# Spreading small vectors over the partitions of a four-layer graph network: through DRAM in place of transposes of repeated columns

## The chip, the cores and the metric

The kernel runs on one core of a Trainium2 chip. The metric is the device time of one execution in microseconds (us). Before the change it is 2883.72 us, the median of three runs (2882.16 to 2886.92).

A core has five engines with queues of their own: TensorE (PE in the profile; PEld is its weight load), VectorE (DVE), ScalarE (ACT), GpSimd (POOL) and SyncE (SP). Transfers between DRAM and the on-chip memory are issued on the queues of SP, ACT and POOL and carried out by 16 DMA engines.

## The reference

Four layers over 2708 nodes with 512 features each, all with the same adjacency `adj` (2708 x 2708, mostly zeros), in float32. Each layer adds its result to x and normalises the rows. What the change touches belongs to the first two:

```python
# layer 0: incidence = adj
mask = adj > 0
head = mask / maximum(sqrt(sum(mask * mask, axis=-1)), EPS)   # 1/sqrt(count of the row)
inc = adj + head
x = layernorm(x + (inc @ x) / sum(inc, axis=-1))
# layer 1
h = x @ W_sa
s_left, s_right = h @ a_sa[0, :512], h @ a_sa[0, 512:]        # = x @ (W_sa @ a)
attn_a = sigmoid(concat([adj @ x, x]) @ Wa.T + ba)            # attn_b alike, with Wb
e = where(adj != 0, exp(-leaky_relu(s_left[:, None] + s_right[None, :])), 0)
x = layernorm(x + sigmoid(attn_a * ((e / sum(e)) @ h) + attn_b * (adj @ (x @ W_gcnb) + b_gcnb)))
```

So layer 0 needs for each node the inverse root of its count of neighbours, and adds it to each entry of its row that is not zero. Layer 1 needs four scalar products of every node's x with fixed vectors: two score vectors (W_sa times the halves of a_sa) and the second halves of Wa and Wb.

## The kernel before

The adjacency is held transposed (`adjT`), so that a node's row is a column on the chip: 128 source nodes on the partitions, a range of target nodes along the free axis. Each product adj @ x is one level of a seven-product scheme on halves of 1354 nodes. A **sweep** goes over ranges of target nodes; for layer 0 these are (768,256), (0,384), (384,384) and (1024,330) (start within a half, length), numbered 0 to 3 here. For each range the four blocks 11, 21, 22 and 12 of `adjT` are loaded as tiles of 128 x n (SP queue, L394), combined by DVE into sums (L403; stored for later layers by POOL, L406), and multiplied on PE (L458, with the rest of the rows at L467 to L482) by parts of x: B11, B22, B21 and the sums T1 to T4 (L224 to L232), each in groups A to D of three tiles. Results gather in PSUM banks, of which there are eight under one tag.

**Order.** Nothing is issued where it stands in the code. Every step is put down as an event, `at(position, function)`; a sweep takes 28 positions per layer (`S[1]` is where layer 1's begins), and the events run sorted by position. A scheduler then moves instructions of each engine after a start-up stretch. On one queue everything runs in its order: an issue that waits holds what stands behind it. Tiles come from rings (38 for adjacency tiles, 17 called tmp, 6 masks), and a tile is overwritten when its last reader is done.

**Counts and inverse roots (layer 0).** For the next range, `count_load` (L691) loads 22 tiles per half again, on SP for range 1 and on POOL for ranges 2 and 3, ACT (L712, L713) or DVE (L710) makes masks of them, and PE multiplies each mask by a column of ones (`count_tile`, L723), so that the counts gather with the target nodes on the partitions, one column for each 128. `count_row` (L728) makes the inverse root y of them on DVE and ACT (L735 to L743, tile "r"). The entries are needed along the free axis, the same on all partitions, because DVE adds them to tiles that have the target nodes there. So `spread_row` (L746) takes each column of y, repeated 128 times along the free axis, as a matrix and transposes it on PE (L751, tile "pr"), and ACT copies the result to the tile "row" (L754). `prep0` uses it (L769, L770). Each range has two halves, h = 0 and 1, each with a spreading of its own: three transposes, or two for range 0.

**Score vectors (layer 1).** `start0` loads W_sa and the halves of a_sa, and DVE multiplies and adds them up (L842) into `vmat`, [128, 4 chunks, 4 vectors]; L845 adds the columns of Wa and Wb. Just after layer 1's sweep begins (position S[1] + 0.85), `spread_v` (L891) makes each of the 16 columns, repeated, into a 128 x 128 matrix, transposes it on PE (L897, tile "pv", four PSUM banks), and ACT copies the banks into eight 128 x 256 tiles (L900) that lie in parts of the x groups B and D that no product needs any more: B11B, B22B, T1B, T2B, T3B, B21B, B11D, B22D. `score` (L904) multiplies each tile of the new x with them on DVE (L909).

`to_rows` (L920) is an existing helper of layer 1: it transposes a few columns on PE (L923, tile "ps_r"), copies the rows on ACT (L925, tile "rows") and stores them to DRAM on POOL's queue (L926). The rows s_left so stored are read back for all partitions by SP (L1075). At the start of layer 1's sweep, the last tiles of layer 0's result are still being finished: PE transposes them back (L589, tile "ps_n"), DVE adds them to x (L824) and normalises (L553 to L567), which writes the parts of B11 that layer 1's first products read.

Of the kernel before, what the change touches and what calls it, by code (L numbers as in the profile page):

```python
# [21 lines left out]
F32 = mybir.dt.float32  # L22
# [3 lines left out]
P = 128  # L26
# [4 lines left out]
RANGES0 = [(768, 256), (0, 384), (384, 384), (1024, 330)]  # L31
# [27 lines left out]
def wt(k):  # L59
    return min(P, NH - k * P) if k < KT else P  # L60
# [8 lines left out]
def gnn_kernel(ctx: ExitStack, tc: tile.TileContext, x, adjT, w_sa, a_sa, w_gcn, b_gcn, wab, bab, w_hop, w_out,  # L69
               b_out, out):  # L70
    nc = tc.nc
    N, D = x.shape
    NT = 2 * KT
    DC = D // P
    HD = D // 2
    assert N == 2 * NH and D == 512

    const = ctx.enter_context(tc.tile_pool(name="const", bufs=1))
    feat = ctx.enter_context(tc.tile_pool(name="feat", bufs=1))
    pool = ctx.enter_context(tc.tile_pool(name="pool", bufs=1))  # L80
    small = ctx.enter_context(tc.tile_pool(name="small", bufs=6))
    psum = ctx.enter_context(tc.tile_pool(name="psum", bufs=1, space=bass.MemoryType.PSUM))
    dram = ctx.enter_context(tc.tile_pool(name="dram", bufs=1, space=bass.MemoryType.DRAM))

    ident = const.tile([P, P], F32, name="ident")
# [23 lines left out]
    wab_sb = const.tile([P, 2 * DC, 2], F32, name="wab_sb")  # L109
# [5 lines left out]
    for c in range(1, DC):  # L115
        nc.vector.tensor_tensor(pick, pick, ident[:, 32 * c : 32 * c + 2], ALU.add)
    bab_sb = const.tile([P, 2], F32, name="bab_sb")
    vmat = const.tile([P, DC, 4], F32, name="vmat")
    sc = const.tile([P, NT, 4], F32, name="sc")
    sc2 = const.tile([P, NT, 2, 4], F32, name="sc2")  # L120
    nc.vector.memset(sc2, 0.0)
# [1 line left out]
    def feature(nm):  # L123
# [6 lines left out]

    SROW = {(R0, h): dram.tile([(w + P - 1) // P, P], F32, name=f"SR{R0}_{h}", tag=f"SR{R0}_{h}")
            for R0, w in RANGES for h in range(2)}
    DROW = [dram.tile([1, KT * P], F32, name=f"DR{h}", tag=f"DR{h}") for h in range(2)]

    X2T = {(g, h): dram.tile([D, 2 * n], F32, name=f"X2T{g}_{h}", tag=f"X2T{g}_{h}")
# [6 lines left out]
    def bcast(src, n):  # L142
        return bass.AP(tensor=src.tensor, offset=src.offset, ap=[[0, P], [1, n]])
# [12 lines left out]
    def tmp(nm):  # L156
        return pool.tile([P, 384], F32, name=nm, tag="tmp", bufs=NTMP)
# [10 lines left out]
    def bank(nm, shape=None):  # L168
        return psum.tile(shape or [P, D], F32, name=nm, tag="x", bufs=8)
# [6 lines left out]
    def at(pos, fn, hold=False):  # L176

        def go():
            n = len(nc.cur_bb.bb.instructions)
            fn()  # L180
            held.update(range(n, len(nc.cur_bb.bb.instructions)))

        events.append((pos, len(events), go if hold else fn))
# [499 lines left out]
    S = [28.0 * s for s in range(8)]  # L683


    row, run, rd = {}, {}, {}
    cnt = {}
    V = {}

    def tiles_of(R0, n):  # L690
        return list(range(R0 // P, (R0 + n + P - 1) // P))  # L691

    def count_load(R0, n, h, i):
        w = wt(i % KT)
        t = tmp("cl")
        j0 = (i // KT) * NH + (i % KT) * P

        move(nc.sync if R0 == RANGES0[1][0] else nc.gpsimd, t[:w, :n], adjT[j0 : j0 + w, h * NH + R0 : h * NH + R0 + n])
        cnt[R0, h, i] = t

    def count_rows(R0, i):

        return {KT - 1: KA, NT - 1: 32}.get(i, P) if R0 == RANGES0[0][0] else wt(i % KT)
# [22 lines left out]
    def count_row(R0, n, h):  # L726


        ts = tiles_of(R0, n)
        r = small.tile([P, 4, 4], F32, name="r", bufs=2)  # L730
        ps = cnt.pop(h)
        if wt(ts[-1]) < P:
            nc.vector.memset(r[:, 0, :], 1.0)
        for j, q in enumerate(ts):
            nc.vector.tensor_scalar(r[: wt(q), 0, j : j + 1], ps[: wt(q), j : j + 1], 1.0, None, ALU.max)  # L735
        m = len(ts)

        c, y, q, t = (r[:, i, :m] for i in range(4))
        nc.scalar.activation(q, c, AF.Sqrt)
        nc.vector.reciprocal(q, q)  # L740
        nc.vector.tensor_tensor(t, q, q, ALU.mult)
        nc.vector.scalar_tensor_tensor(t, c, -0.5, t, ALU.mult, ALU.mult)
        nc.vector.scalar_tensor_tensor(y, t, 1.5, q, ALU.add, ALU.mult)  # L743
        cnt[R0, h] = r

    def spread_row(R0, n, h):  # L746
        r = cnt.pop((R0, h))
        pr = bank("pr")
        for j, q in enumerate(tiles_of(R0, n)):
            w = wt(q)  # L750
            nc.tensor.transpose(pr[:, q * P - R0 : q * P - R0 + w], r[:w, 1, j : j + 1].to_broadcast([w, P]),  # L751
                                ident[:w, :w])
        row[R0, h] = tmp("row")
        nc.scalar.copy(row[R0, h][:, :n], pr[:, :n])  # L754
# [30 lines left out]
    def extra0(pb, r, R0, n, A):  # L785
        if r == 0:
            for h, p, d in ((0, -3.7, 0.05), (1, 1.9, 0.055)):
                for j, i in enumerate([*range(KW), *range(KT, KT + KW), KT - 1, NT - 1]):
                    key = (f"{h + 1}{i // KT + 1}", i % KT) if i % KT < KW else ("r" if i < KT else "r32", h)
                    a = lambda key=key: A[(0,) + key]  # L790
                    at(pb + p + d * (j - 2 * h), lambda h=h, i=i, a=a: count_mask(R0, n, h, i, a(), h == 0 or i % KT == KT - 1))
                    at(pb + p + d * j, lambda h=h, i=i: count_tile(R0, n, h, i))
                    at(pb + (1.7 if h == 0 else 4.8) + 0.06 * j,
                       lambda h=h, i=i, a=a: add_run(R0, h, n, count_rows(R0, i), a()))
                at(pb + p + d * 22, lambda h=h: count_row(R0, n, h))
                at(pb + p + d * 22 + 0.1 * h, lambda h=h: spread_row(R0, n, h))
        if r + 1 < len(RANGES0):
            R1, n1 = RANGES0[r + 1]
            for h, p, d in ((0, 1.0, 2.5), (1, 3.8, 2.5)) if r else ((0, 3.2, 2.2), (1, 5.4, 2.1)):
                for i in range(NT):  # L800
                    q = pb + p + d * i / NT
                    at(q - 0.7, lambda i=i, h=h: count_load(R1, n1, h, i))
                    at(q - 0.35, lambda i=i, h=h: count_mask(R1, n1, h, i))
                    at(q, lambda i=i, h=h: count_tile(R1, n1, h, i))
                at(pb + p + d, lambda h=h: count_row(R1, n1, h))
                at(pb + p + d + 0.15, lambda h=h: spread_row(R1, n1, h))

        def inverse(o, s, t, w):
            nc.vector.reciprocal(o, s)

        at(pb + (5.2 if r else 3.3), lambda: run_sums(R0, n, 0, inverse))
        at(pb + (4.7 if r else 6.4), lambda: run_sums(R0, n, 1, inverse))
# [20 lines left out]
    def start0():  # L833
        ws = load_w(w_sa)
        nc.scalar.dma_start(out=wab_sb, in_=wab)
        nc.scalar.dma_start(out=bab_sb, in_=bcast(bab, 2))
        y = nat("vy")
        for n in range(2):
            v = nat("va")
            nc.scalar.dma_start(out=v, in_=bcast(a_sa[:, n * D : (n + 1) * D], D))  # L840
            for c in range(DC):
                nc.vector.scalar_tensor_tensor(y, ws[c], 1.0, v, ALU.mult, ALU.mult,  # L842
                                               accum_out=vmat[:, c, n : n + 1])
        for c in range(DC):
            nc.vector.tensor_copy(vmat[:, c, 2:4], wab_sb[:, DC + c, :])  # L845
            nc.vector.tensor_copy(wab_pad[:, c, 0:2], wab_sb[:, c, :])

    def x0_load(k, s):
# [7 lines left out]
    for k in range(KW):  # L856
        f = k / KT
# [33 lines left out]
    def spread_v():  # L891

        homes = [spare_part(s, g) for g in "BD" for s in ("B11", "B22", "T1", "T2", "T3", "B21")][:8]
        for j in range(4):
            ps = bank("pv")
            for c in range(DC):
                nc.tensor.transpose(ps[:, c * P : (c + 1) * P], vmat[:, c, j : j + 1].to_broadcast([P, P]), ident)  # L897
            for e in range(2):
                V[j, e] = homes[2 * j + e]
                nc.scalar.copy(V[j, e], ps[:, e * HD : (e + 1) * HD])  # L900

    at(S[1] + 0.85, spread_v)

    def score(t, w, got):  # L904
        x1 = got[t]
# [6 lines left out]
    def scores_end(R0, h, ts):  # L912
# [3 lines left out]
        nc.vector.tensor_copy(s_right[:, q], sc[:, q, 1])  # L916
        for j in range(2):
            nc.vector.tensor_scalar(gate_x[:, q, j], sc[:, q, 2 + j], bab_sb[:, j : j + 1], None, ALU.add)

    def to_rows(cols, m, dst):  # L920

        ps = bank("ps_r", [P, P])
        nc.tensor.transpose(ps[:m], cols, ident)  # L923
        t = small.tile([P, P], F32, name="rows", bufs=2)
        nc.scalar.copy(t[:m], ps[:m])  # L925
        nc.gpsimd.dma_start(out=dst, in_=t[:m])  # L926

    def score_rows(R0, h, ts):
        q = slice(h * KT + ts[0], h * KT + ts[-1] + 1)
# [24 lines left out]
    def extra1(pb, r, R0, n, A):  # L954
# [32 lines left out]
        def rows(h):  # L987
            to_rows(rdeg[:, h * KT + ts[0] : h * KT + ts[-1] + 1], len(ts),
                    DROW[h][0, ts[0] * P : (ts[-1] + 1) * P].rearrange("(k i) -> k i", i=P))

# [450 lines left out]
    def finish_degrees():  # L1441
        t = small.tile([24, P], F32, name="fd", bufs=1)
        nc.vector.memset(t, 1.0)
        for g, (i0, n) in enumerate(RANGES2):
            for h in range(2):
                for s in range(2):
                    r, a = 12 * g + 6 * h + 3 * s, i0 + s * n
                    nc.gpsimd.dma_start(out=t[r : r + 2], in_=DROW[h][0, a : a + 2 * P].rearrange("(k i) -> k i", i=P))
                    nc.gpsimd.dma_start(out=t[r + 2 : r + 3, : n - 2 * P], in_=DROW[h][0:1, a + 2 * P : a + n])
        ps = bank("ps_r", [P, 24])  # L1450
# [104 lines left out]
    for n, i in enumerate(list(nc.cur_bb.bb.instructions)):  # L1555
        p = last if n < 3 * strict else done if n in held else {}
# [44 lines left out]
```

## Time and profile before

| | |
|---|---|
| median of three runs | 2883.72 us |
| profiled execution | 2883.33 us |
| its span (first to last instruction) | 2881.2 us |
| mean granted TensorE clock | 0.998 |
| PE busy | 2832.7 us, 98% |
| DVE busy | 2195.9 us, 76% |
| ACT, POOL busy | 550.1 us, 617.6 us |
| moved by DMA | 510.04 MB, mean 177 GB/s |
| transposes "pr" (L751) | 22, of 273 ns median |
| copies "row" (L754) | 8, of 449 ns median |
| transposes "pv" (L897) | 16, of 273 ns median |
| copies of "pv" (L900) | 8, of 372 to 453 ns |
| transposes "ps_r" (L923) | 16, of 272 ns median |

The profile is of one execution. The duration of a matmul includes the time until its result is out, and matmuls overlap; so the time that one takes from the next is read from their starts. A timeline's line is a run of alike instructions: start, length from the first start to the last end, engine, line, operation, output, inputs, shape and number, and in brackets how long the engine was idle before it, and for whom. Layer 0's sweep lies at about 10 to 440 us, with its ranges in order; layer 1's follows, until about 830.

### The profile page before, as it was taken

How to read it: one execution, taken by the hardware profiler on the slowest of the kernel's cores; microseconds unless marked ns; L12 is line 12 of the kernel's file. 1: busy time of each engine (PE TensorE's matmuls, PEld its weight loads, DVE VectorE, ACT ScalarE, POOL GpSimd, SP SyncE). 2: the span in 40 equal slices, each digit the busy share in tenths (PEclk: the TensorE clock that was granted, in tenths of full speed). 3: DMA queues.
4: the chain of work that ended last, by engine and by line, in shares of the span. 5: the costliest groups of instructions: out<-in, count | busy, mean ns of one | idle time of the engine just before them, and what ended most of it. 6: DMA issues, size and time to landing. Idle time of an engine off the chain costs nothing. (4 is left out here: it accounts for less than half of the span.)

```text
span 2881.2 us, 37482 instructions
## 1 busy us (share of the span) xinstructions
PE 2832.7 (98%) x10963; PEld 1870.3 (65%) x10963; DVE 2195.9 (76%) x5670; ACT 550.1 (19%) x1119; POOL 617.6 (21%) x1113
## 2 busy tenths in 40 slices
PE   7999999999999999999999999999999999999998
PEld 5655665657765656866666666666666666666665
DVE  6898798576736464654699787887878877799987
ACT  4544200111136444542100000000000100100001
POOL 0123223123320101122203123031230211501202
PEclk9999999999999999999999999999999999999999
DMA  7665466354544333565667767566675666754542
GB/s 229 193 212 179 133 204 218 124 181 143 183 140 130 117 113 98 151 198 151 195 205 236 213 192 246 166 201 208 187 250 168 181 197 182 230 174 145 175 142 92
DMA packets 368524, 510.04 MB, mean 177 GB/s; under 512 B 63424, under 2 KB 321700, under 8 KB 368320
## 3 DMA queue, kind: packets, MB, share of 16 engines
q1 hardware_dynamic: 302392, 370.56, 43.5%
q0 software_dynamic: 49344, 126.38, 13.1%
q10 hardware_dynamic: 16584, 10.71, 1.3%
q8 instruction: 87, 1.43, 0.2%
q14 instruction: 117, 0.96, 0.1%
HBM read 423.77 MB, written 83.65 MB: 176 GB/s over the span
## 5 line engine op out<-in xcount | busy, mean ns | idle before, releaser
L1212 DVE TENSOR_TENSOR z<-z 128x339 f32<-128x339 f32 (+1 forms) x966 | 454.3, 503 | 12.5 <-PE accu L1267 3.2
L1285 ACT COPY q<-accu 128x338 f32<-128x338 f32 (+1 forms) x84 | 34.6, 443 | 1003.3 <-PE accu L1267 806.0
L560 POOL TENSOR_TENSOR rstd<-rstd,neg_half 128x1 f32<-128x1 f32 (+3 forms) x91 | 59.3, 652 | 762.2 <-DVE rstd L559 516.6
L1267 PE MATMUL accc<-s,t 128*128 128x338 f32 (+1 forms) x644 | 198.1, 450 | 0.0
L1267 PE MATMUL accu<-z,t 128*128 128x338 f32 (+1 forms) x644 | 194.0, 448 | 1.5 <-DVE z L1212 1.5
L1267 PE MATMUL accd<-z,t 128*128 128x338 f32 (+1 forms) x644 | 193.9, 448 | 0.6 <-DVE q L1349 0.6
L1267 PE MATMUL accc<-z,t 128*128 128x338 f32 (+1 forms) x644 | 193.5, 448 | 0.5 <-ACT q L1285 0.5
L1400 POOL DMA_DIRECT2D Y<-y x192 | 105.1, 554 | 366.3 <-DVE y L1395 333.3
L403 DVE TENSOR_TENSOR a<-a,a 128x384 f32<-128x384 f32 (+2 forms) x330 | 162.4, 510 | 23.1 <-PE accu L458 22.4
L1267 PEld LDWEIGHTS accc<-s,t 128*128 128x128 f32 x644 | 120.9, 190 | 64.1 <-issue 7.5
L1267 PEld LDWEIGHTS accc<-z,t 128*128 128x128 f32 x644 | 122.0, 190 | 61.6 <-issue 1.0
L1267 PEld LDWEIGHTS accu<-z,t 128*128 128x128 f32 x644 | 121.7, 190 | 61.7 <-DVE z L1212 2.0
L1267 PEld LDWEIGHTS accd<-z,t 128*128 128x128 f32 x644 | 121.9, 190 | 60.5 <-DVE q L1349 1.5
L1212 DVE TENSOR_TENSOR s<-z 128x338 f32<-128x338 f32 (+1 forms) x322 | 149.7, 503 | 12.7 <-PE accc L1267 8.4
L1291 DVE TENSOR_TENSOR q<-q,accd 128x338 f32<-128x338 f32 (+1 forms) x112 | 56.0, 500 | 115.2 <-PE accd L1267 115.2
L1068 DVE SCALAR_TENSOR_TENSOR a<-a,e 128x384 f32<-128x384 f32 (+2 forms) x160 | 77.4, 507 | 49.8 <-ACT e L1067 49.5
L1066 ACT ACTIVATE e<-row,s_right 128x384 f32<-128x384 f32 (+5 forms) x176 | 96.3, 569 | 76.2 <-PE accc L458 20.4
L965 DVE SCALAR_TENSOR_TENSOR deg<-a,deg 128x384 f32<-128x384 f32 (+2 forms) x152 | 75.2, 505 | 19.0 <-DMA a<-in_adjT 17.9
L406 POOL DMA_DIRECT2D As<-a x120 | 64.9, 544 | 82.3 <-DVE a L403 80.3
L1067 ACT ACTIVATE e<-e 128x384 f32<-128x384 f32 (+5 forms) x176 | 79.3, 477 | 1.8
L606 PE MATMUL ps_d<-w,xT 128*128 128x512 f32 (+1 forms) x176 | 79.2, 593 | 0.4 <-ACT xT L597 0.4
L769 DVE SCALAR_TENSOR_TENSOR s<-a,row 128x384 f32<-128x384 f32 (+2 forms) x152 | 75.0, 505 | 6.0 <-ACT row L754 6.0
(683 smaller groups left out, 5869.0 us busy)
## 6 DMA issues: line engine op xcount, KB each, us to landing
z<-As SPq DMA_DIRECT2D x320, 169.5 KB
z<-As SPq DMA_DIRECT2D x320, 169.0 KB
a<-in_adjT SPq DMA_DIRECT2D x240, 192.0 KB
z<-in_adjT SPq DMA_DIRECT2D x240, 169.5 KB
z<-in_adjT SPq DMA_DIRECT2D x240, 169.0 KB
a<-in_adjT SPq DMA_DIRECT2D x120, 165.0 KB
a<-in_adjT SPq DMA_DIRECT2D x112, 128.0 KB
As<-a POOLq DMA_DIRECT2D x60, 192.0 KB, 4.2
```

Source lines behind the costliest of these rows:

```text
L403: nc.vector.tensor_tensor(A[r, dst, k][:, :n], A[r, a, k][:, :n], A[r, b, k][:, :n], op)
L406: nc.gpsimd.dma_start(out=SD[m][k * P : (k + 1) * P, R0 : R0 + n], in_=A[r, dst, k][:, :n])
L560: nc.gpsimd.tensor_tensor(rstd[:w, 1:2], rstd[:w, 0:1], neg_half[:w], ALU.pow)
L606: nc.tensor.matmul(o, lhs(c), r, start=c == 0 and n == 0, stop=c == DC - 1, skip_group_check=True)
L769: nc.vector.scalar_tensor_tensor(t[:w, :n], a[:w, :n], 0.0, row[R0, h][:w, :n], ALU.is_gt, ALU.mult)
L965: nc.vector.scalar_tensor_tensor(d[:w, :n], a[:w, :n], 0.0, d[:w, :n], ALU.not_equal, ALU.add)
L1066: nc.scalar.activation(e[:w, :n], row[R0, h][:w, :n], AF.Prelu, bias=s_right[:w, t : t + 1], alpha=0.01)
L1067: nc.scalar.activation(e[:w, :n], e[:w, :n], AF.Exp, scale=-1.0)
L1068: nc.vector.scalar_tensor_tensor(a[:w, :n], a[:w, :n], 0.0, e[:w, :n], ALU.not_equal, ALU.mult)
L1212: nc.vector.tensor_tensor(d[:, :n], Z[x + (k,)][:, :n], Z[y + (k,)][:, :n], op)
L1267: nc.tensor.matmul(B[home][:, :n], stat(v, k), a[:, :n], start=bool(start and k == 0), stop=k == nk - 1, skip_group_check=True)
L1400: nc.gpsimd.dma_start(out=rows[:, :, f * P : (f + 1) * P], in_=o[32 * f : 32 * (f + 1), : m * P].rearrange("p (b d) -> p b d", d=P))
```

## The change

`vmat` is laid out by vector, then chunk. `to_rows` may be given a queue and is defined earlier. Two DRAM tiles are added.

- The four vectors' 16 columns are transposed in one piece, at position 10.3, soon after `start0`, and stored as 16 rows on POOL's queue. `spread_v`, now at S[1] + 0.75, issues eight loads on SP's queue, each of which reads half a vector (256 numbers) for all 128 partitions into the tile that ACT's copy wrote before.
- For the first halves (h = 0) of ranges 1 to 3, `row_out` transposes the three columns of the inverse roots in one piece and stores three rows on ACT's queue, at the position where `spread_row` was, and `row_in`, 0.45 positions later, reads them for all partitions on SP's queue. The second halves, and both halves of range 0, stay with `spread_row`.
- `count_row` sets all of the tile "r" to 1 for a range that ends in a tile of under 128 nodes, where it set only the counts.

```diff
-    vmat = const.tile([P, DC, 4], F32, name="vmat")
+    vmat = const.tile([P, 4, DC], F32, name="vmat")
...
+    VROW = dram.tile([4 * DC, P], F32, name="VR", tag="VR")
+    CROW = {R0: dram.tile([3, P], F32, name=f"CR{R0}", tag=f"CR{R0}") for R0, _ in RANGES0[1:]}
...
-            nc.vector.memset(r[:, 0, :], 1.0)
+            nc.vector.memset(r, 1.0)
...
+    def to_rows(cols, m, dst, queue=None):
+
+        ps = bank("ps_r", [P, P])
+        nc.tensor.transpose(ps[:m], cols, ident)
+        t = small.tile([P, P], F32, name="rows", bufs=2)
+        nc.scalar.copy(t[:m], ps[:m])
+        (queue or nc.gpsimd).dma_start(out=dst, in_=t[:m])
+
+    def row_out(R0, n, h):
+        r = cnt.pop((R0, h))
+        m = len(tiles_of(R0, n))
+        to_rows(r[:, 1, :m], m, CROW[R0][:m, :], nc.scalar)
+
+    def row_in(R0, n, h):
+        src = CROW[R0][0:1, :]
+        row[R0, h] = tmp("row")
+        nc.sync.dma_start(out=row[R0, h][:, :n], in_=bcast(src, n))
...
-                at(pb + p + d + 0.15, lambda h=h: spread_row(R1, n1, h))
+                if h:
+                    at(pb + p + d + 0.15, lambda h=h: spread_row(R1, n1, h))
+                else:
+                    at(pb + p + d + 0.15, lambda h=h: row_out(R1, n1, h))
+                    at(pb + p + d + 0.6, lambda h=h: row_in(R1, n1, h))
...
-                                               accum_out=vmat[:, c, n : n + 1])
+                                               accum_out=vmat[:, n, c : c + 1])
...
-            nc.vector.tensor_copy(vmat[:, c, 2:4], wab_sb[:, DC + c, :])
+            nc.vector.tensor_copy(vmat[:, 2:4, c], wab_sb[:, DC + c, :])
...
-            ps = bank("pv")
-            for c in range(DC):
-                nc.tensor.transpose(ps[:, c * P : (c + 1) * P], vmat[:, c, j : j + 1].to_broadcast([P, P]), ident)
+            src = VROW[j * DC : (j + 1) * DC, :]
             for e in range(2):
                 V[j, e] = homes[2 * j + e]
-                nc.scalar.copy(V[j, e], ps[:, e * HD : (e + 1) * HD])
-
-    at(S[1] + 0.85, spread_v)
+                nc.sync.dma_start(out=V[j, e], in_=bass.AP(tensor=src.tensor, offset=src.offset + e * HD, ap=[[0, P], [1, HD]]))
+
+    at(10.3, lambda: to_rows(vmat.rearrange("p j c -> p (j c)"), 4 * DC, VROW))
+    at(S[1] + 0.75, spread_v)
```

More of the change, by code (lines that the diff above doesn't have):

```diff
@@ L918, in scores_end @@
             nc.vector.tensor_scalar(gate_x[:, q, j], sc[:, q, 2 + j], bab_sb[:, j : j + 1], None, ALU.add)
[L920 to L926, printed above, removed]
     def score_rows(R0, h, ts):
```

## The prediction

> **What bounds the kernel now.** I read the busy shares first, then what TensorE (PE) waited for, then PE's stretches around the touched places, and only then the queues.
>
> The page's busy part, first rows:
>
> ```profile
> span 2881.2 us, 37482 instructions
> PE 2832.7 (98%) x10963; PEld 1870.3 (65%) x10963; DVE 2195.9 (76%) x5670; ACT 550.1 (19%) x1119; POOL 617.6 (21%) x1113
> ```
>
> PE is busy 98% of the span: a microsecond taken from PE's stream is a microsecond gained, unless PE then waits longer; work on other engines and queues is free until it makes PE wait. The waits of PE (engine, line, waited for: us, times, longest) name the two places that this change touches:
>
> ```profile
> PE pr L751 <- DVE r L743: 5.8, 3, 2.7
> PE accu L458 <- DVE B11D L567: 3.1, 2, 2.1
> ```
>
> The first is the wait for an inverse root, before the transposes that spread it; the longest of the three (2.7) is range 1's first half. The second stands right behind the transposes of the score vectors, as PE's timeline shows:
>
> ```profile
> 441.68 4.03 PE L458 MATMUL accu<-a,B11C 128*128 128x384 f32 x12
> 445.55 1.91 PE L897 MATMUL pv<-ident,vmat 128*128 128x128 f32 x16
> 449.53 1.56 PE L458 MATMUL accu<-a,B11D 128*128 128x384 f32 x4 [2.06 <-DVE B11D L567]
> ```
>
> PE ends the sixteen transposes at 447.46, then idles 2.06 us until VectorE (DVE) has written B11D. Who makes B11D late is in DVE's timeline:
>
> ```profile
> 444.31 0.56 DVE L965 SCALAR_TENSOR_TENSOR deg<-a,deg 128x384 f32<-128x384 f32 x1 [6.41 <-DMA a<-in_adjT]
> ...
> 449.06 0.41 DVE L567 TENSOR_SCALAR B11D<-ld,mv,rstd 128x256 f32<-128x256 f32 x1
> ```
>
> DVE stands idle 6.41 us for one adjacency tile, and runs without a break from its landing to B11D. No transpose of the score vectors is in this chain.
>
> The third thing to see is the granted clock (start:end, us, PE, PEld, DVE, ACT and POOL busy, PEclk, DMA share, GB/s) around the 2.73 us wait at 89.42 to 92.14:
>
> ```profile
> 90.00:91.00 1.00, 0.00 (x0) 0.00 (x0) 0.96 (x5) 0.10 (x1) 0.00 (x0) 0.92 0.96 315
> 91.00:92.00 1.00, 0.00 (x0) 0.00 (x0) 0.63 (x5) 0.88 (x3) 0.00 (x0) 0.50 0.60 187
> ...
> 96.00:97.00 1.00, 1.00 (x7) 0.64 (x5) 1.00 (x4) 0.97 (x3) 0.00 (x0) 0.50 0.70 183
> 97.00:98.00 1.00, 1.00 (x5) 0.87 (x4) 1.00 (x4) 0.89 (x2) 0.00 (x0) 0.67 0.42 128
> ```
>
> The clock falls to 0.50 about 1.4 us into the idle time (0.92 in the first slice) and stays there some 6.8 us (0.16 + 6 + 0.66). PE works 5.5 of these at half rate, so it loses 2.75 us beside the wait itself. The 2.06 us wait at 447 costs no clock: the slice 445.5 to 449.5 has 1.00.
>
> **What goes.** PE loses 25 transposes. The three groups of the first halves (ranges 1, 2, 3) stand at 92.14, 178.14 and 284.25. At 178.14 three take 0.33 us until the next matmul (0.11 each); at 92.14, at half clock, 0.70. So 0.70 + 0.33 + 0.33 = 1.36 us leave PE. The sixteen at 445.55 take 16 x 0.11 = 1.76 us, but the next matmul waits for B11D, which does not depend on them: their going only lengthens the wait from 2.06 to about 3.85 us (445.68 to 449.53). I count 0. ScalarE (ACT) loses 11 copies of 0.37 to 0.48; it is at 19%, so 0.
>
> **What comes on PE.** Four transposes of 2 to 16 columns (one for each range, one for all score vectors). The nearest rows, the same helper's for degrees and scores, last 0.27 us each, drain included; the time a transpose takes from the next matmul is 0.11, as above (0.22 at half clock). 0.22 + 3 x 0.11 = 0.55, bounds 0.45 and 1.1. I take 0.55. Each still waits for the same root or vector: range 1's wait stays 2.73 us, with its slow clock; the vectors' last product ends on DVE at 173.58, and the transpose's place in the built order is about 174.27, so 0.7 us of cover; without cover, up to the row of such a wait, 2.7.
>
> **The clock behind the longer wait.** A wait of 3.85 us is longer than the 2.73 that halved the clock. Bounds: 0 (as after 2.06) and 2.75 (as after 2.73). If the clock falls 1.4 us into the wait for 6.8 us, it is low from 447.1 to 453.9. The four matmuls from 449.53 take 2.6 us instead of 1.3, until 452.1; but PE stood idle from 451.09 to 452.09 there for the next B11D, so that is hidden. From 452.1 to 453.9, 1.8 us at half rate lose 0.9. I take +0.9. [...]
>
> **What comes on the queues.** Three ACT-issued stores, one POOL-issued store, eleven loads on SP (three rows of 165 to 192 KB, eight vector halves of 128 KB): 1.6 MB of 510, on DMA engines busy 58%. Small stores of the same helper land in 1.5 / 1.8 / 5.4 us (least, median, most). What counts is that a queue is in order: an issue that waits holds everything behind it. I went through the changed kernel's instruction order place by place, with the old times:
> - Range 1's row load stands on SP ahead of eight count loads (issued 87.63 to 96.5). The root comes at 92.1, so the round trip ends about 95.5, and SP stands some 8 us. The loads then go out by about 100.6; their masks start on ACT from 104.68: 4 us of cover. The row is first used at 102.51, and lands near 99.
> - Ranges 2 and 3: SP stands 2.6 us at 179.7 and under 1 us at 286; users start 1.5 us or more later.
> - The vectors' store makes POOL stand from about 161.5 to 175.5, ahead of four count loads issued at 164 to 166 before. They land about 180 to 181; ACT needs them from 183.1. Cover 2 to 3 us.
> - Each vector half overwrites a tile that PE still reads, so SP waits for PE. The longest is the first: B11B waits from about 336.4 to 347.14, 10.7 us, with some ten issues behind it (338.6 to 349.96, to go out by 352.4); DVE uses them from 352.66 on, cover 2 to 5 us, and PE uses DVE's output later still. Others (T1B, T2B, B22B, B22D, B21B) move loads by 0.6 to 4.4 us, with users 4 us or more behind.
>
> I take 0 for all of them: PE has no wait on a DMA there, and SP waits of 20.3 us (longest of 82 on one line) are in the profile with PE at 98%. Without cover, each costs what PE's waits for DVE cost in the rows above, 1.0 to 2.7 us.
>
> **One wait moves by itself.** SP's transfers take completion counters in turn, shared with ACT's, and wait for the one before on the same counter. At 434.57 SP stood for that:
>
> ```profile
> SPq L297 <- DMA B11R<-X: 4.1, 1, 4.1
> ```
>
> The added transfers shift whose turn it is. By the new order the tile that DVE waits for at 444.31, issued at 435.25, waits for a transfer that lands about 438.5. It landed 9 us after its issue, behind a full DMA load, so 3.3 us later at issue are less at landing: between -1 (other loads are out of its way) and +3. I take +0.5, since the backlog in front of it, not its issue, set its time.
>
> **Sum**, against the profiled execution (2883.33 us, span 2881.2): 2883.33 - 1.36 + 0.55 + 0.9 + 0.5 = **2883.9**. The median shown is 2883.72, so this is no difference that can be seen: about 0.2%, 5.8 us, is what a measurement of this kernel can tell from no change.
>
> **Rivals.**
> - *Faster: the tile lands early.* If DVE's tile comes 4 us sooner, B11D is ready when PE gets there: 3.85 us of wait go, the clock stays up, and with -0.81 the time is 2883.33 - 3.85 - 0.81 = 2878.7; if range 1's slow clock is avoided as well (2.75), 2875.9. For it: the chain is set by that one landing. Against: the tile is issued later, not earlier. 0.20, of which 0.12 past 0.2%.
> - *Slower: SP's wait for PE at the vector halves.* If tiles held behind B11B, T1B, T2B, B22B and B22D land after DVE wants them, PE starves by 1.0 to 2.7 us at each (the bounds above): five times 1.8, about 9, with PE then at work where the slow clock was counted (0.9), gives 2883.9 - 0.9 + 9 = 2892. It decides from the point where a held tile takes over 2 us (the thinnest cover) from issue to landing; the small stores' most is 5.4, the tile above took 9. Against: PE has DVE's output in hand. 0.22, of which 0.18 past 0.2%.
> - *Nothing changes*: all of it is hidden, the clock too: 2883.33 - 0.81 = 2882.5. 0.08.
> - Forecast: 0.50, own range 2881 to 2888.
>
> **Numbers.** Faster 0.12; same 0.50 + 0.08 + 0.08 + 0.04 = 0.70; slower 0.18. The range runs from 2877.5 (into the faster case) to 2891 (into the slower one), leaving about 0.1 on each side.
>
> **What would show it.** Right: no pr groups at 178 and 284, accu behind 445.7 idle 3 to 4 us for B11D, a granted clock near 0.5 in 450 to 454, and no new wait of PE between 340 and 430. Wrong: PE waiting on DVE a (L403, L770) with DVE waiting on DMA there (slower rival); B11D early (faster rival); a wait at the score transpose near 174 or for a count mask near 183; clock 1.00 behind the long wait.

## The result, and the profile after

The changed kernel takes 2887.64 us (median of 20 runs, 2884.27 to 2893.5); the kernel before, timed beside it, 2883.44 us (median of 20, 2877.94 to 2886.92). The ratio is 1.0015, with a 95% interval of 1.0009 to 1.0021: 0.15% slower, 2.6 to 6.1 us. The profiled execution took 2888.78 us. All profiled spans below are single executions, and one kernel's differ by several us; so times are compared by ratios, and profiles by the waits that they show.

The page's busy part after the change:

```profile
span 2887.0 us, 37440 instructions
PE 2834.3 (98%) x10942; PEld 1869.5 (65%) x10942; DVE 2195.7 (76%) x5670; ACT 548.4 (19%) x1112; POOL 617.4 (21%) x1114
```

PE has 21 matmuls fewer, and is busy 1.6 us longer: some of its work ran at a lower clock (mean granted 0.996, for 0.998 before). Its waits (engine, line, waited for: us, times, longest):

```profile
PE ps_n L591 <- DVE P1c L521: 4.6, 1, 4.6
PE accu L460 <- DVE B11D L569: 3.5, 1, 3.5
...
PE ps_r L751 <- DVE r L745: 2.7, 1, 2.7
PE accd L460 <- DVE a L405: 2.5, 3, 1.9
```

The longest wait for a root (ps_r) is as long as the one for pr was: a row is now one small transpose, behind the same wait. The wait for B11D grew. The longest, for P1c, is one that the prediction does not mention. It was there before, at 2 us, as PE's timeline of the kernel before shows:

```profile
436.14 0.74 PE L589 MATMUL ps_n<-ident,P1c 128*128 128x128 f32 x2 [1.98 <-DVE P1c L519]
```

After the change, the same work and what follows:

```profile
439.71 0.88 PE L591 MATMUL ps_n<-ident,P1c 128*128 128x128 f32 x2 [4.58 <-DVE P1c L521]
...
454.14 5.49 PE L460 MATMUL accu<-a,B11D 128*128 128x384 f32 x8 [3.53 <-DVE B11D L569]
```

The eight matmuls behind B11D take 5.49 us, where two groups of four took 1.56 each before. The clock is the reason (start:end, us, PE, PEld, DVE, ACT, POOL busy, PEclk, DMA share, GB/s):

```profile
440.00:441.00 1.00, 1.00 (x5) 0.88 (x5) 1.00 (x4) 0.00 (x0) 0.26 (x2) 0.50 0.46 130
...
453.00:454.00 1.00, 0.00 (x0) 0.00 (x0) 0.85 (x2) 0.00 (x0) 0.56 (x1) 0.55 0.00 0
...
457.00:458.00 1.00, 1.00 (x3) 0.54 (x2) 0.87 (x3) 0.00 (x0) 0.95 (x2) 0.50 0.39 152
...
459.00:460.00 1.00, 1.00 (x2) 0.46 (x2) 0.54 (x2) 0.33 (x1) 0.53 (x1) 0.53 0.08 16
```

It is halved behind both waits: 3.4 us long behind the first (0.28 x 2 + 2 + 0.43 x 2, from the slices 439 to 443), 6.8 us behind the second.

Who makes P1c late? DVE's timeline before, and then after, at the sum that needs the third tile of B22's group C:

```profile
420.80 0.42 DVE L225 TENSOR_TENSOR T2C<-B22C,T1C 128x256 f32<-128x256 f32 x1 [0.26 <-DMA B22C<-X]
```

```profile
358.94 0.50 DVE L789 SCALAR_TENSOR_TENSOR s<-a,row 128x330 f32<-128x330 f32 x1 [1.10 <-DMA a<-in_adjT]
...
424.37 0.43 DVE L227 TENSOR_TENSOR T2C<-B22C,T1C 128x256 f32<-128x256 f32 x1 [2.86 <-DMA B22C<-X]
...
439.16 0.90 DVE L521 TENSOR_TENSOR P1c<-P1c,acca 128x330 f32<-128x330 f32 x2
...
448.92 0.56 DVE L980 SCALAR_TENSOR_TENSOR deg<-a,deg 128x384 f32<-128x384 f32 x1 [7.12 <-DMA a<-in_adjT]
```

DVE waits 1.10 us for an adjacency tile that it never waited for, and 2.6 us longer for B22C. From there on it runs into P1c with no pause but one of 0.46 us, which it had before as well. The tile B22C is loaded by POOL, whose issues come 0.96 us later (417.77 for 416.81), as everything does behind the first wait; from issue to landing (least, median, most) it took, before and after:

```profile
DMA to landing us min/median/max: 2.7/2.9/2.9
```

```profile
DMA to landing us min/median/max: 5.1/5.5/5.5
```

And SP stands where the prediction said, by its own waits after the change between 336 and 372:

```profile
SPq L922 <- PE accu L460: 10.7, 1, 10.7
SPq L922 <- PE accd L460: 6.8, 1, 6.8
```

**Where the time came from.** The start of the same matmul in both profiles, after minus before, tells where PE falls behind. It is +0.48 at 58 us (from the first loads, not the change) and -0.16 at 340: -0.19 is a shorter wait for DVE at 58, and -0.45 comes between 60 and 340, where the groups of pr went and the small transposes came. From there:

| place on PE | after - before | step |
|---|---|---|
| 340 | -0.16 | |
| T1C, behind DVE's 1.10 us wait at 358.9 | +0.97 | +1.13 |
| ps_n, wait for P1c | +3.57 | +2.60 |
| accu B11B, slow clock behind it | +4.90 | +1.33 |
| accu B11D, behind DVE's tile at +4.61 | +4.61 | -0.29 |
| accc T3B, slow clock behind it | +6.20 | +1.59 |
| ps_r of the degrees, whose wait of 0.60 goes | +5.44 | -0.76 |
| last matmul | +5.58 | +0.14 |

The steps are PE's, and not each is a cost. DVE's tile in front of B11D (the line at 448.92, 444.31 before) came 4.61 us later, and it alone sets when B11D is ready: the 1.33 us of the slow clock behind P1c only made PE's wait for it shorter.

### The profile page after: what moved, and what is told of

Same layout as the page of the kernel before. It is cut to its first block, busy times and chain, and to the rows that moved or that the text cites. A ratio compares the mean times of both kernels' runs of the same rounds, so it can differ in the third digit from the quotient of the medians.

```text
span 2887.0 us, 37440 instructions
## 1 busy us (share of the span) xinstructions
PE 2834.3 (98%) x10942; PEld 1869.5 (65%) x10942; DVE 2195.7 (76%) x5670; ACT 548.4 (19%) x1112; POOL 617.4 (21%) x1114
## 5 line engine op out<-in xcount | busy, mean ns | idle before, releaser
L1227 DVE TENSOR_TENSOR s<-z 128x338 f32<-128x338 f32 (+1 forms) x322 | 149.6, 503 | 10.7 <-PE accc L1282 8.2
```

What stands on the lines that cost most here:

```text
L1227: nc.vector.tensor_tensor(d[:, :n], Z[x + (k,)][:, :n], Z[y + (k,)][:, :n], op)
```

## The experiments

Theory: (1) the score vectors' loads among layer 0's last loads make B22C and adjacency tiles late, through SP's hold, their bytes or both; (2) the missing transposes only lengthen the wait for B11D; (3) behind a longer wait the clock is halved. Rivals: the rows' round trips are the loss; or PE's work counts and the loss is something else. Each kernel ran 8 to 11 times beside 15 to 30 runs of the kernel before on the same chip; ratios are to that.

**Only the rows** (twice). In the changed kernel:

```diff
-            src = VROW[j * DC : (j + 1) * DC, :]
+            ps = bank("pv")
+            for c in range(DC):
+                nc.tensor.transpose(ps[:, c * P : (c + 1) * P], vmat[:, j, c : c + 1].to_broadcast([P, P]), ident)
...
-                nc.sync.dma_start(out=V[j, e], ...)
+                nc.scalar.copy(V[j, e], ps[:, e * HD : (e + 1) * HD])
...
-    at(10.3, lambda: to_rows(vmat.rearrange("p j c -> p (j c)"), 4 * DC, VROW))
-    at(S[1] + 0.75, spread_v)
+    at(S[1] + 0.85, spread_v)
```

> The rows of the first halves through DRAM as in the change; the score vectors by transposes as before. My theory now (the loss lies with the score vectors' loads and with the slow clock behind longer waits; the rows are worth a little): time 0.5 us below before, ratio 0.9998; PE's waits at 436 and 449 as before (about 2.0 and 2.1), clock 1.00 behind them. Rival (the rows' round trips hold the queues and cost the time): 3 to 5 us above before, with the waits at 436 and 449 as long as after the change (4.6 and 3.5).

> The variant with only the rows through DRAM, a second time, since it came out 3.4 us faster than before (interval 0.9 to 6.1) where my terms gave 0.5. If that is so: ratio again near 0.9988. [...]

Ratios 0.9988 (0.9979 to 0.9997) and 0.9992 (0.9983 to 1.0000): faster than before, by 3.5 and 2.3 us in the middle, the second 0.0004 above what was expected. P1c's wait is 2.3 and 2.1 us. The rival is out: the rows are no loss. The gain is larger than my 0.5 us, which the second interval takes in and the first (from 0.9 us) just does not. The two profiles of this one kernel differ by 4.9 us of span, and show why a single profile cannot settle it. The clock near range 1, first profile, then second:

```profile
85.00:86.00 1.00, 1.00 (x6) 0.77 (x5) 0.97 (x4) 0.97 (x4) 0.00 (x0) 0.50 1.03 320
...
94.00:95.00 1.00, 1.00 (x9) 0.80 (x8) 0.93 (x4) 0.97 (x3) 0.00 (x0) 1.00 0.24 77
```

```profile
85.00:86.00 1.00, 1.00 (x9) 0.80 (x8) 0.97 (x4) 0.97 (x3) 0.00 (x0) 1.00 0.98 343
...
94.00:95.00 1.00, 1.00 (x4) 0.73 (x3) 0.93 (x4) 0.97 (x3) 0.00 (x0) 0.50 0.20 69
```

In one the clock fell behind the wait of 2.02 us at 81 and stayed up behind the one at 89, which was only 1.82 us long there; in the other it stayed up behind 2.02 us and fell behind 2.74 us at 88, for twice as long. In the second it also fell for 6.8 us behind the wait for B11D (2.83 us), against the expectation of 1.00 there.

**Only the score vectors.** The changed kernel with `spread_row` for all halves.

> The score vectors through DRAM as in the change; all rows by transposes as before. My theory: 4 to 5.5 us above before, ratio about 1.0017; DVE waits about 1 us for an adjacency tile near 358 and 2 to 3 us for B22C near 421, PE waits over 4 us for P1c near 436 and over 3 us for B11D, and the granted clock is 0.5 behind both. Rival (the rows are the loss): within 1 us of before, or 1 to 2 below it.

Ratio 1.0031 (1.0020 to 1.0042), 9 us: more than expected, and enough for all of the loss. The profile is of a run of 2897.0 us, above the median of 2891.71. DVE waited 3.0 us for B22C, PE 4.7 us for P1c and 4.7 for B11D, and the clock was 0.50 behind both.

**Fifteen of the sixteen transposes taken from the kernel before.**

```diff
-            ps = bank("pv")
-            for c in range(DC):
-                nc.tensor.transpose(ps[:, c * P : (c + 1) * P], vmat[:, c, j : j + 1].to_broadcast([P, P]), ident)
+        # once, ahead of the loop over j
+        ps = bank("pv")
+        nc.tensor.transpose(ps[:, :P], vmat[:, 0, 0:1].to_broadcast([P, P]), ident)
...
-                nc.scalar.copy(V[j, e], ps[:, e * HD : (e + 1) * HD])
+                nc.scalar.copy(V[j, e], ps[:, 0:1].to_broadcast([P, HD]))
```

> The kernel before, with one of the sixteen transposes of the score vectors; the eight copies spread that one result, so fifteen of the sixteen columns are left out. No transfer is added. My theory (these transposes stand in a wait that something else ends): the wait for B11D grows from 2.1 to about 3.7 us, and the time stays or grows by up to 2.7 us, by the slow clock behind the longer wait (granted clock 0.5 for some 3 to 7 us from about 449). Rival (PE is busy 98%, so its work counts): 1.65 us below before (15 x 0.11).

Ratio 0.9997 (0.9988 to 1.0006): no gain is seen, though the interval would hold one of 1.65 us (0.9994), so the time alone decides nothing. The profile shows where the work went, in PE's timeline and the clock:

```profile
445.76 0.27 PE L895 MATMUL pv<-ident,vmat 128*128 128x128 f32 x1
451.03 5.38 PE L458 MATMUL accu<-a,B11D 128*128 128x384 f32 x8 [5.00 <-DVE B11D L567]
```

```profile
452.00:453.00 1.00, 1.00 (x3) 0.51 (x2) 0.41 (x3) 0.00 (x0) 0.87 (x2) 0.50 0.84 61
```

The wait took the work's place (of its 5.00 us some 1.3 are because B11D came later in this execution), and the clock fell to 0.50 behind it, with no transfer added.

**The transposes put back into the changed kernel, unread.**

```diff
+            ps = bank("pv")
+            for c in range(DC):
+                nc.tensor.transpose(ps[:, c * P : (c + 1) * P], vmat[:, j, c : c + 1].to_broadcast([P, P]), ident)
             src = VROW[j * DC : (j + 1) * DC, :]
```

> The changed kernel, with the sixteen transposes put back at their old place for PE alone: nobody reads them, and the vectors still come from DRAM. My theory: not slower than the changed kernel though PE does 1.76 us more; the wait for B11D falls from 3.5 to about 1.8 us, the clock behind it stays 1.00, and the time falls by 1 to 2.5 us against the changed kernel (2 to 3.5 us above before). The wait for P1c near 436, over 4 us, and the late B22C stay. Rival (PE's work counts): 1.8 us above the changed kernel, 6 above before.

Ratio 1.0009 (1.0000 to 1.0017), against 1.0015 for the changed kernel. The intervals overlap, so a gain is not shown; a loss of 1.8 us (to 1.0021) is just outside. P1c's wait is still 4.6, but behind B11D the clock stays up:

```profile
455.08 1.56 PE L460 MATMUL accu<-a,B11D 128*128 128x384 f32 x4 [1.42 <-DVE B11D L569]
457.52 1.56 PE L460 MATMUL accu<-a,B11D 128*128 128x384 f32 x4 [0.89 <-DVE B11D L569]
```

**The vectors' loads kept at their place in the list**, on SP behind layer 0's last loads (the third argument keeps the scheduler from moving an event's instructions):

```diff
-    at(S[1] + 0.75, spread_v)
+    at(S[1] + 0.75, spread_v, True)
```

> The changed kernel, with the eight loads of the score vectors kept at their place in the list of events, after the last tiles of layer 0's end on SP's queue, so that SP does not wait for PE between 336 and 430 and none of these loads is under way with B22C. My theory (the loads among layer 0's last loads make B22C and the adjacency tile late): DVE's wait for B22C under 1 us, PE's wait for P1c about 2, no clock loss there; what is left is the longer wait for B11D with a slow clock behind it; 1 to 3 us above the variant that has only the rows, so -2.5 to +1 us against before. Rival (the missing transposes before the wait for B11D are the whole loss, by the clock): about as the changed kernel, +4.

Ratio 0.9996 (0.9987 to 1.0005): the loss is gone. B22C lands after 2.9 us again, DVE waits 0.3 for it, and what is left is the longer wait and a slow clock behind it:

```profile
PE accu L460 <- DVE B11D L569: 4.6, 1, 4.6
PE ps_n L591 <- DVE P1c L521: 2.0, 1, 2.0
```

```profile
450.00:451.00 1.00, 1.00 (x2) 0.42 (x2) 0.40 (x2) 0.00 (x0) 0.88 (x2) 0.50 0.74 235
```

**The same, with the transposes put back, unread** (the edit as above).

> The variant with the vectors' loads kept at their place, with the sixteen transposes put back at their old place for PE alone, unread. My theory (the clock falls behind the longer wait): PE's wait for B11D falls from 4.6 to about 2.8 us or is split in two, the clock stays 1.00 or is slow for fewer us behind it, and the time is the same or up to 1.5 us lower though PE does 1.76 us more. Rival (PE's work counts): 1.76 us higher.

Ratio 0.9998 (0.9989 to 1.0007): 1.76 us more PE work, no difference that can be seen, though the intervals would hold one of that size. The clock is 1.00 from 446 to 452, behind waits of 2.83 and 0.89 us.

**Is it the one place in DRAM, the queue, or the bytes?** Three kernels. The vectors' rows stored sixteen times, and read from sixteen places:

```diff
-    VROW = dram.tile([4 * DC, P], F32, name="VR", tag="VR")
+    VROW = dram.tile([16, 4 * DC, P], F32, name="VR", tag="VR")
...
-                nc.sync.dma_start(out=V[j, e], in_=bass.AP(..., ap=[[0, P], [1, HD]]))
+                nc.sync.dma_start(out=V[j, e], in_=bass.AP(..., ap=[[4 * D, 16], [0, 8], [1, HD]]))
...
+        nc.gpsimd.dma_start(out=VROW.rearrange("r q i -> q r i"), in_=t[: 4 * DC].unsqueeze(1).to_broadcast([4 * DC, 16, P]))
```

> The changed kernel, with the vectors' rows stored sixteen times in DRAM, so that a load of one half reads sixteen different places and not one for all 128 partitions. If reading one place 128 times is what holds up B22C: DVE's wait for it falls from 2.9 to under 1 us, PE's wait for P1c from 4.6 to about 2, and the time falls by 2 to 4 us against the changed kernel (0 to 2 above before). If it is only that these and the held loads come just then: as the changed kernel, 4 to 5 us above before, with waits of 2.9 and 4.6.

Ratio 1.0024 (1.0014 to 1.0035), B22C after 5.3 us, DVE's wait 2.7, P1c's 4.4, as in the changed kernel: not the one place.

The loads on ACT's queue:

```diff
-                nc.sync.dma_start(out=V[j, e], ...)
+                nc.scalar.dma_start(out=V[j, e], ...)
```

> The changed kernel, with the eight loads of the score vectors on ACT's queue instead of SP's, at about the same times (ACT then waits for PE, and its own later work waits behind). If it is SP's hold that hurts (the loads behind it come late and close together): DVE's wait for B22C falls under 1 us, its waits for adjacency tiles near 358 go, PE's wait for P1c is about 2, and the time is near that of the variant with loads kept at their place (ratio about 0.9996 to 1.0005). If it is the vectors' transfers themselves, under way with B22C: that wait stays 2 to 3 us, P1c's over 4, and the time stays 3 to 5 us above before.

Ratio 1.0009 (1.0000 to 1.0018), DVE's wait for B22C 1.7, P1c's 3.4: between the two expectations. SP no longer waits for PE at the vector halves, and part of the lateness stays. B22C from issue to landing:

```profile
DMA to landing us min/median/max: 4.3/4.5/4.7
```

The separation is not clean: from 342.4 to 350.2 SP stood 7.8 us for the landing of the vector half in B11B that ACT had issued (the kind of wait that the prediction quoted for B11R).

The hold without the bytes, in the variant with only the rows:

```diff
+        for t in homes:
+            nc.sync.dma_start(out=t[:, 0:8], in_=bcast(a_sa[:, 0:8], 8))
...
-    at(S[1] + 0.85, spread_v)
+    at(S[1] + 0.75, spread_v)
```

> The variant with only the rows (score vectors by transposes), and at the eight places in SP's queue where the changed kernel loads the vectors, a load of 8 columns (4 KB instead of 128) into the same tiles, so that SP waits for PE in the same places and almost nothing is transferred; the transposes' copies then overwrite them. If SP's hold is what makes B22C and the adjacency tiles late: B22C lands 4 to 5.5 us after its issue, DVE waits 1.5 to 3 us for it, PE waits over 3 us for P1c, and the time is 3 to 6 us above the variant without these loads. If it is the bytes of the vectors: B22C lands after about 2.9, P1c's wait is about 2, and the time is within 1.5 us of that variant (ratio to before 0.9988 to 0.9998).

Ratio 1.0006 (0.9997 to 1.0015), against 0.9988 and 0.9992 without these loads: 4 to 5 us in the middle (some 0.5 to 9 by the intervals), for eight loads of 4 KB. SP waits as in the changed kernel (10.7 and 7.1 us for PE), and DVE and PE behind it:

```profile
423.46 0.42 DVE L227 TENSOR_TENSOR T2C<-B22C,T1C 128x256 f32<-128x256 f32 x1 [1.46 <-DMA B22C<-X]
```

```profile
PE ps_n L591 <- DVE P1c L521: 3.2, 1, 3.2
PE accu L460 <- DVE B11D L569: 1.8, 2, 0.9
```

B22C lands after 4.0 us. So of the 2.6 us that B22C is later in the changed kernel, SP's hold without the bytes makes 1.1, and the bytes with the hold on ACT's queue 1.6, by one execution of each: both count. SP's timeline shows one way from the hold to B22C. Two loads of x go out some 3 us ahead of B22C's first issue (416.81) in the kernel before:

```profile
413.54 0.50 SPq L149 DMA_DIRECT2D ld<-in_x  x1
414.09 0.50 SPq L151 DMA_DIRECT2D ld<-in_x  x1
```

With the 4 KB loads they stand behind one that waits 3.4 us for PE, and go out among B22C's issues (from 418.27):

```profile
418.77 0.51 SPq L151 DMA_DIRECT2D ld<-in_x  x1
419.33 0.50 SPq L153 DMA_DIRECT2D ld<-in_x  x1
```

The changed kernel has the same (418.28 and 418.84, beside 417.77); with the loads on ACT's queue they stay ahead (413.91 and 414.46, beside 417.18). Whether these two loads are the whole of the 1.1 us was not separated. Near 356, DVE is late by 1.8 us with the 4 KB loads and by 0.7 with the loads on ACT's queue, but stands for POOL's rstd there, not for a tile; in the first of the two POOL itself stood 3.69 us for a store of x to land, 1.00 before.

**The second halves' rows too.** `row_out` and `row_in` (0.05 positions behind it) for h = 1 as well, in the variant with only the rows.

> As the variant with only the rows, but the second halves of ranges 1 to 3 too (three more round trips, nine transposes fewer and three small ones more). If a row through DRAM gains by PE's work alone: 0.7 us below the variant with the first halves (6 x 0.11). If the second halves' shorter time before use makes DVE wait: DVE waits for a DMA ahead of L789 near 120, 225 and 335, PE waits behind it, 1 to 3 us at each, and it is 2 to 8 us slower than the variant with the first halves.

Ratio 1.0026 (1.0017 to 1.0035), some 10 us above the variant with the first halves, more than the 2 to 8 expected. The round trip is too long there, by DVE's and then PE's waits between 100 and 420:

```profile
DVE s L789 <- DMA row<-CR: 13.5, 3, 7.9
```

```profile
PE accd L460 <- DVE a L405: 9.6, 3, 7.8
```

**Work for the clock in range 1's wait**, in the variant with only the rows:

```diff
         ps = bank("ps_r", [P, P])
+        for _ in range(fill):          # 20 for range 1
+            nc.tensor.transpose(ps, ident, ident)
         nc.tensor.transpose(ps[:m], cols, ident)
```

> The variant with only the rows, with twenty transposes of the identity, unread, ahead of the small transpose of range 1, into its own bank: 2.2 us of PE work in the wait of 2.7 us at 89. [...] Rival (the slow clock there costs nothing that shows, or the transposes delay the root's own): same or up to 2.2 us slower than the variant without them.

Of the wait 0.57 us is left behind the filling, and the clock is 1.00 from 85 to 100:

```profile
89.05 2.35 PE L752 MATMUL ps_r<-ident 128*128 128x128 f32 x20
91.97 0.27 PE L753 MATMUL ps_r<-ident,r 128*3 128x128 f32 x1 [0.57 <-DVE r L745]
```

```profile
90.00:95.00 5.00, 4.43 (x35) 3.71 (x34) 4.38 (x16) 3.66 (x9) 0.00 (x0) 1.00 0.01 5
...
435.00:436.00 1.00, 1.00 (x3) 0.34 (x2) 0.00 (x0) 0.00 (x0) 0.87 (x2) 0.50 0.74 246
```

The time shows no gain: 0.9996 (0.9987 to 1.0004), no faster than without the filling (0.9988 and 0.9992). In the profile the clock stays up at 90, and falls at 434 instead, behind a wait of 2.1 us; the kernel before waited 1.98 us there and kept 1.00. I do not know what the filling costs elsewhere. A saving of 1 to 2.8 us, my estimate from slow spells of 3.4 and 6.8 us at half rate, is not seen; set against the two runs of the variant without it, the intervals leave room for about 1.4 at most. The variant with only the rows stays the fastest in the middle.

## Why the prediction was right, and where it failed

The range (2877.5 to 2891) held the time, and the forecast of no visible difference did. The sum said +0.6, the runs +4.3 (2.6 to 6.1), so the size rests on terms that were missing. That even the narrower range of the forecast alone (2881 to 2888) held 2887.64, near its top, is in part luck: 3.7 us of it came by a path that the sum had at 0. Point by point:

- **The pv transposes worth 0**: right, and shown in the profiles, where the wait takes the place of the fifteen, and gives place to the sixteen put back; the times (0.9997, 1.0009 against 1.0015, 0.9998 against 0.9996) show no gain of one or loss of the other, though the first and the last pair would not show one of 1.7 us.
- **The longer wait and the clock, +0.9**: right in kind; +1.59 in the profile, with the kept loads the longer wait and a slow clock, 3.4 us long, are what is left. The bounds of 0 and 2.75 held it.
- **The pr transposes, -0.81**: right. From their starts to the next matmul's, the three groups took 0.70, 0.33 and 0.29 us (the sum had 0.33 for the last too), the four small transposes 0.17, 0.11, 0.11 and 0.10: -0.83. The profile has only -0.45 by 340, mainly because the slow clock reached farther into PE's work behind range 1's wait: the matmuls from 92.97 to 98.30 before took 5.33 us, the same ones after 5.66 (92.75 to 98.41). By ratios the rows gain 0.08 and 0.12%, more than the profile accounts for. What else is gained there stays open.
- **"I take 0 for all of them"**, of the queues: this step failed. Its ground was that PE has no wait on a DMA there and that long SP waits hide elsewhere. But the chain goes from SP to a load, from it to DVE, from DVE to PE, and DVE made up for nothing between 358 and 439: the 1.10 us at 358.9 and the 2.6 at 421 reach PE whole, as steps of 1.13 and 2.60, where the sum had 0. The prediction's own sign of the slower rival is there: PE's wait for DVE's a at 372 grew from 1.09 to 1.92 us, with DVE waiting for a DMA. The tile of 358.9 was issued at 345.69 before and at 352.32 after, as the prediction had it, 5.5 us ahead of its user; but it took 6.6 us to land. I had set the covers against issue times and a landing of about 2 us. And B22C, on POOL's queue, was on no list of mine, though its landing went from 2.9 to 5.5 us beside what SP had under way. Eight loads of 4 KB in the same places cost 4 to 5 us; that is the slower rival's cause (SP's wait for PE at the vector halves), at half its price of 9, but its larger part came through B22C, which SP does not load. The point from which it decides was named ("over 2 us" from issue to landing), and the rows beside it, 5.4 and 9 us, said that it would be passed.
- **The moved wait, +0.5**: right in kind, 1.04 in the profile, inside the bounds of -1 and 3. DVE's tile landed 4.61 us later, P1c was 3.57 late. The 3.57 reach the tile too: POOL stored DVE's last rows 3.57 us later (429.74, then 433.31), ACT issued its load of B11R when that store had landed (432.36, then 435.76), and SP stood for B11R, a longer form of the wait that the prediction quoted, and then once more for B22R (both below). So the tile was issued 5.68 us later (435.25, then 440.93); of what goes beyond the 3.57, half was left at its landing. In the trace of the kernel before, the 2390 transfers of SP and ACT report their landing on eight counters, 298 or 299 of them on each, and all but nine wait for their own counter first; SP's issue at 434.57 waits for the one of ACT's load of B11R from 432.36.
- **A second slow clock**, behind the wait for P1c, was not foreseen. It held PE back by 1.33 us and cost nothing in the end, since PE then waited for DVE's tile all the same: at B11D, -0.16 + 1.13 + 2.60 + 1.04 = 4.61 without it. The prediction did not follow P1c's wait, though with 2 us it was already the second longest of the stretch.

SP's own waits ahead of DVE's tile, after the change:

```profile
SPq L153 <- DMA B11R<-X: 8.4, 1, 8.4
SPq L396 <- DMA B22R<-X: 1.8, 1, 1.8
```

The length of the wait alone does not tell whether the clock falls: behind 1.92 us at 372 it stayed at 1.00 in the changed kernel, and was 0.50 behind 1.9 us there with the transposes put back; behind 2.8 us for B11D it stayed at 1.00 with the loads kept and the transposes put back, and was 0.50 in the second profile with only the rows.

## What to carry to other kernels

Before work is taken from a busy engine, look at what ends the wait behind it: here the work that stood in a wait was free (0.9997 without fifteen of the sixteen transposes), and in the profiles it even kept the clock up (1.00 behind B11D with the sixteen put back, 0.50 without). A load that must wait for its buffer belongs behind the loads that need not wait on its queue (0.9996 so, 1.0015 ahead of them); a cover has to be looked up for every transfer in flight, on all queues, up to the first engine that has no reserve. And where the clock falls behind a wait in one execution and not in another (2.02 us at 81, with only the rows), a few us are settled by medians of many runs, not by two profiles.

## What was not expected of the hardware

- The clock of the same kernel, in two executions, fell behind different waits of 2.0 to 2.8 us, for 3.4 or 6.8 us; past 300 us it was 0.50 behind eleven waits of 3.2 to 7.8 us, for P1c, B11D or DVE's a, in nine profiles.
- Loads of B22C that POOL issued at the same rhythm landed after 2.9, 4.0, 4.5 or 5.5 us, by what SP and ACT had under way; eight loads of 4 KB that held SP were enough for 1.1 of it.
- Reading one DRAM place for 128 partitions or sixteen copies of it made no difference that shows (5.5 and 5.3 us for B22C beside it).
